# The gate's two experts by two maxima instead of by ranks from all pairs

## The chip, the core and the metric

The kernel runs on one core of one Trainium2 chip. The metric is the device time of one execution in microseconds, as the median of the runs shown. Engines are named as the profile names them: PE is TensorE, DVE is VectorE, ACT is ScalarE, POOL is GpSimd, SP is SyncE, whose queue carries nearly all DMAs.

## The reference

Two layers act on an input of 8 x 256 x 32 x 32 (8 images of 1,024 tokens with 256 channels). Layer 0 is a selective state-space scan over 512 channels with 16 states, and then a mixture of experts: for each token a gate gives probabilities over 8 experts, and the two largest choose the experts and weight their outputs. Layer 1 has three small convolutions and a second, smaller scan, and then a feed-forward network on the half of the tokens that a router ranks highest. The part that the change concerns:

```python
logits = xf @ gate_w + gate_b
probs = jax.nn.softmax(logits, axis=-1)
top2_vals, top2_idx = jax.lax.top_k(probs, 2)
cw = jnp.zeros((N, Ee), dtype=xf.dtype).at[jnp.arange(N)[:, None], top2_idx].add(top2_vals)
```

`top_k` takes the expert with the lower index where two probabilities are equal.

## The kernel before

Layer 0's scan is cut into 16 units, each one image half (512 tokens); four units are a group of 2,048 tokens. A unit is normalized, projected and convolved (`norm`, `project`, `rows_of`, `dt_of`), and then scanned (`scan_unit`, which calls `scan_pair` for every pair of states and each block of 128 channels). One `scan_pair` is, for two states: one POOL multiplication of 128x1024 (L821), two exponentials on ACT into PSUM (L826), two scans along the tokens on DVE (L829), two copies of the last column on ACT (L833, where a half follows), two DVE multiplications (L834), in some pairs a POOL addition (L838), and the sums on PE (L845). The rows `bc` that it multiplies by come by DMA from DRAM, spread over all partitions; there are four buffers for them.

After a unit's scan, `tokens` projects back, takes statistics and writes the gate's logits for its 512 tokens (with small POOL operations, L955 to L964). After each fourth unit, `route` works on the 2,048 tokens of the group. They lie as 128 partitions x 16 blocks, with 8 expert columns each: a tile of 128x128, `[P, NB, E]`. `route` makes a softmax (L983 to L992), finds the two experts of each token (`better` and `masks`, L997 to L1016), counts tokens by expert on PE (`counts`, L1021), gives each token a slot for each of its experts (`sums`, `ends`, `ends2`, `pick`), and turns the gate weights for the bias sum (`chosen`, L1081). All of its tiles lie in one buffer of 1,024 columns, `r`, through the helper `small`. Columns 384 to 767 hold three masks of 128 columns: `sel` (either of the two), `sel1` (the first) and `sel2` (the second).

`better` compares, for two blocks at a time (hence 8 parts), each of the 8 probabilities of a token with each of the other 8: greater than, equal, equal and of lower index (by the constant `first`), the sum of both, and the sum over the others, which is the rank. `masks` makes rank below 1.5, rank below 0.5, and their difference. All of it is on DVE.

Behind a routing come, for its group, `scatter` (token rows to their slots by indirect DMA from POOL, L1113), `experts` (23 blocks of 256 slots, with two DMAs of weights for each block, L1172, and matmuls L1202 and L1224), `combine` (gathers by POOL's indirect DMA, L1300, and the weighted sum), and then layer 1: `taps_of`, `mamba_in`, `mamba_scan` (`scan_pair` again), `mamba_out`, `assemble`, `ranks`, `feed_forward` and `finish`. The work of one group overlaps the scans of later units. For the last group nothing is left to overlap with but the group before it.

The order on every engine is made by a planner when the kernel is built (`Flow`). Each step is declared with `step(engine, us, prio, run, reads, writes, ...)`: an estimated cost, a priority, and the buffers that it reads and writes. The planner picks step after step by priority among those that are ready by its own clock, and hands out buffers from pools; the priorities of later stages come from a table, `PLAN`. Where PE would stand idle for over 0.7 us by this clock, `warm` puts up to eight multiplications by a tile of zeros there (L560 and L564), about one for each 0.3 us. The engines then run their instructions in that order.

Of the kernel before, what the change touches and what calls it, by code (L numbers as in the profile page):

```python
# [31 lines left out]
ALU = mybir.AluOpType  # L32
AX = mybir.AxisListType
# [3 lines left out]
P = 128  # L37
# [5 lines left out]
E, HE = 8, 512  # L43
# [4 lines left out]
NB = 16  # L48
# [46 lines left out]
PE, ACT, DVE, POOL, SP = "PE", "ACT", "DVE", "POOL", "SP"  # L95
# [100 lines left out]
class Flow:  # L196
# [6 lines left out]
    def step(self, engine, us, prio, run, reads=(), writes=(), fills=(), claims=(), table=None, lat=0.0, scan=False):  # L203


        bufs = list(dict.fromkeys([*reads, *writes, *fills, *claims]))
        fresh = list(dict.fromkeys([*writes, *fills, *claims]))
        s = Step(engine, us * (PACE if engine == PE else 1.0), prio, run, table, lat, bufs, fresh)
        for b in fresh:
            b.first = min(b.first, (prio, len(self.steps)))  # L210
        s.scan = scan
        for b in reads:
            assert b.writers or b.slot is not None, "read before it is written"
            s.needs.update(b.writers)
        for b in writes:
            s.needs.update(b.writers, b.readers)
        for b in reads:
            b.readers.append(s)
        for b in (*writes, *fills):
            b.writers.append(s)  # L220
        for b in bufs:
            b.left += 1
        self.steps.append(s)
        return s
# [96 lines left out]
def layers(g, ctx, x, a, out):  # L321
    tc, nc = g.tc, g.nc
    w = ctx.enter_context(tc.tile_pool(name="w0", bufs=1))
# [66 lines left out]
    gsum = g.t(w, [P, 1, E], "gsum")  # L390


    first = g.t(w, [P, E, E], "first")
    nc.gpsimd.memset(first, 0.0)
    for e in range(1, E):
        nc.gpsimd.memset(first[:, e, :e], 1.0)

    earlier = g.t(w, [P, P], "earlier")
    nc.gpsimd.memset(earlier, 1.0)
    nc.gpsimd.affine_select(  # L400
# [9 lines left out]

    count = g.t(w, [P, NX], "count")
    nc.vector.tensor_tensor_scan(count, ones[:, :NX], ones[:, :NX], -1.0, ALU.mult, ALU.add)

    carry = g.t(w, [P, E, NB], "carry")
    nc.gpsimd.memset(carry, 1.0)
# [49 lines left out]
    step, dma = flow.step, flow.dma  # L465
# [67 lines left out]
    def buf(name, line=None):  # L533
        b = Buf(pool[name], line)
        if line is not None:
            line.bufs.append(b)
        return b
# [16 lines left out]
    wide = still.unsqueeze(1).to_broadcast([P, N // P, P])  # L554
# [413 lines left out]
    def route(n, prio):  # L968

        grp = groups[n]  # L970
        wide = [P, NB, E]
        r, lg = buf("sq"), grp["logits"]

        def small(shape, at):

            dims = " ".join("abc"[: len(shape) - 1])
            size = dict(zip("abc", shape[1:]))
            n = 1
            for m in shape[1:]:
                n *= m  # L980
            return r.v[:, at : at + n].rearrange(f"p ({dims}) -> p {dims}", **size)
# [9 lines left out]
            nc.vector.reciprocal(tot, tot)  # L991
            nc.vector.tensor_tensor(lg.v, lg.v, tot.to_broadcast(wide), ALU.mult)  # L992


        part_of = [P, NB // 8, E, E]

        def better(part):  # L997
            blks = slice(part * NB // 8, (part + 1) * NB // 8)
            gt, eq = small(part_of, 128), small(part_of, 256)
            mine = lg.v[:, blks].unsqueeze(3).to_broadcast(part_of)  # L1000
            other = lg.v[:, blks].unsqueeze(2).to_broadcast(part_of)
            nc.vector.tensor_tensor(gt, other, mine, ALU.is_gt)
            nc.vector.tensor_tensor(eq, other, mine, ALU.is_equal)
            nc.vector.tensor_tensor(eq, eq, first.unsqueeze(1).to_broadcast(part_of), ALU.mult)
            nc.vector.tensor_tensor(gt, gt, eq, ALU.add)
            nc.vector.tensor_reduce(small(wide, 0)[:, blks], gt, AX.X, ALU.add)

        def sels():
            return [small(wide, 384 + 128 * i) for i in range(3)]

        def masks():
            rank = small(wide, 0)
            sel, sel1, sel2 = sels()
            nc.vector.tensor_scalar(sel, rank, 1.5, None, ALU.is_lt)
            nc.vector.tensor_scalar(sel1, rank, 0.5, None, ALU.is_lt)
            nc.vector.tensor_tensor(sel2, sel, sel1, ALU.subtract)  # L1016


        pt, pw = banks(2)
# [66 lines left out]
        step(DVE, 0.4, prio, softmax, [], [r, lg])  # L1086
        step(ACT, 0.25, prio, lambda: nc.scalar.activation(lg.v, lg.v, AF.Exp), [], [lg], table="exp")
        step(DVE, 0.6, prio + 0.5, softmax2, [], [r, lg])
        for part in range(8):
            step(DVE, 1.9, prio + 1 + 0.25 * part, lambda part=part: better(part), [lg], [r])  # L1090
        step(DVE, 0.6, prio + 3, masks, [], [r])
        step(PE, 0.5, prio + 3, counts, [r], [pt])
        step(DVE, 1.7, prio + 3.5, sums, [pt], [r])
        step(DVE, 0.8, prio + 4, ends, [], [r])
# [637 lines left out]
    for i, s in enumerate(UNIT_AT):  # L1732
        if i == 0:
            unit_prep(0)
        dt_of(i, 1, s + 4)
        if i + 1 < len(units):
            fetch_x(i + 1, s)
        scan_unit(i, s)
        if i + 1 < len(units):
            unit_prep(i + 1)  # L1740
        end = s + 2 * DS
        tokens(i, end + 1)
        if i % 4 == 3:
            n = i // 4
            at = PLAN[n]
            route(n, end + 12)
            scatter(n, end + 16, at["put"])
            experts(n, *at["experts"])
            combine(n, *at["combine"])
            taps_of(n, *at["taps"])  # L1750
            m = at["mamba"]
            mamba_in(n, m - 26, m + 5)
            mamba_scan(n, m)
            mamba_out(n, m + DS + 2)
            assemble(n, *at["assemble"])
            ranks(n, at["ranks"])
            feed_forward(n, *at["ffn"])
            finish(n, *at["finish"])
# [4 lines left out]
@with_exitstack  # L1763
def kernel(ctx: ExitStack, tc: tile.TileContext, a: dict, out: bass.AP):
    nc = tc.nc
    g = Ctx(tc)
    const = ctx.enter_context(tc.tile_pool(name="const", bufs=1))
    g.dram = ctx.enter_context(tc.tile_pool(name="dram", bufs=1, space=DRAM))
    g.psum = ctx.enter_context(tc.tile_pool(name="ps0", bufs=1, space=PSUM))
    g.ident = g.t(const, [P, P], "ident")  # L1770
    make_identity(nc, g.ident)
    g.mean256 = g.t(const, [P, P], "mean256")
    nc.gpsimd.memset(g.mean256, 1.0 / C)

    def column(value, tag):
        t = g.t(const, [P, 1], tag)
        nc.gpsimd.memset(t, value)
        return t

    g.one = column(1.0, "one")  # L1780
    g.eps5 = column(1e-5, "eps5")
    g.eps6 = column(1e-6, "eps6")
    g.eps_vim = column(1e-5 * 1e-6, "eps_vim")
    layers(g, ctx, a["x"], a, out)
# [122 lines left out]
```

## Time and profile before

| | us |
|---|---|
| median of 3 runs (lowest to highest) | 3680.02 (3673.19 to 3691.26) |
| the profiled execution | 3683.03 |
| its span | 3681.0 |
| DVE busy | 2918.0 |
| the scans' two DVE lines, L829 and L834, mean of one | 1.22 to 1.28, and 0.69 |
| ACT table loads | 166 of 1.283 |
| granted PE clock, mean | 0.946 |

The four routings begin (first instruction of `softmax`, L985) at 666.7, 1279.8, 1932.2 and 2825.9 us from the start of the span. The last instruction of the fourth (L1083) starts at 2899.2; from 2902 to the end of the span are 779 us. A profile line names the kernel's line, the engine, the operation, what it writes and reads, its shape and its count; then its busy time and mean, and after the bar the time that the engine stood idle just before it.

### The profile page before, as it was taken

The numbers are of one execution on the slowest core, as the hardware profiler recorded it, in microseconds if no ns is written. First come the engines' busy times: TensorE is split into PE (matmuls) and PEld (weight loads), VectorE is DVE, ScalarE is ACT, GpSimd is POOL, SyncE is SP. The second block draws the span as 40 slices with busy tenths as digits, with TensorE's granted clock in tenths as the row PEclk, the third lists the DMA queues.
The fourth block names the chain that finished last, engine by engine and source line by source line (L and its number), as shares of the span: only waits on it lengthen the run. The fifth ranks groups of instructions, "written<-read, shape, count | busy, mean of one in ns | idle before, by whom it ended". The sixth has DMA issues, their size and how long they took to land. (4 is left out here: it accounts for less than half of the span.)

```text
span 3681.0 us, 37497 instructions
## 1 busy us (share of the span) xinstructions
PE 3211.1 (87%) x10567; PEld 1807.2 (49%) x10567; DVE 2918.0 (79%) x4181; ACT 2188.2 (59%) x3985; POOL 2407.4 (65%) x1751
## 2 busy tenths in 40 slices
PE   8889888889889988978998898988888888899858
PEld 3334333334445444444554445555546565685536
DVE  4889889989778987986988789768698938965951
ACT  4555455467567656755875675655675546747533
POOL 3767567487867758986986887654786743716522
PEclk9999999999999999999999999999999988999989
DMA  6334333346445445644654557565657786877756
GB/s 231 132 132 138 110 125 129 107 161 209 159 133 172 167 134 174 203 155 147 211 178 164 179 178 240 190 197 161 195 180 261 234 258 206 307 230 244 265 168 190
DMA packets 276301, 676.61 MB, mean 184 GB/s; under 512 B 31015, under 2 KB 114861, under 8 KB 276094
## 3 DMA queue, kind: packets, MB, share of 16 engines
q1 hardware_dynamic: 257662, 623.87, 51.6%
q0 software_dynamic: 18432, 50.36, 4.2%
q8 instruction: 84, 1.38, 0.2%
q14 instruction: 123, 1.01, 0.1%
HBM read 572.92 MB, written 101.19 MB: 183 GB/s over the span
## 5 line engine op out<-in xcount | busy, mean ns | idle before, releaser
L821 POOL TENSOR_TENSOR dbu<-dtx,bc 128x1024 f32<-128x1024 f32 x551 | 1300.8, 2374 | 239.7 <-PE y L845 119.6
L845 PE MATMUL y<-dbu,ident 128*128 128x512 f32 x1616 | 837.4, 630 | 174.9 <-POOL dbu L838 129.5
L826 ACT ACTIVATE mm<-dt,neg_a 128x512 f32<-128x512 f32 x1152 | 767.7, 688 | 172.9 <-DVE dbu L834 150.6
L829 DVE TENSOR_TENSOR_SCAN mm<-mm,dbu 128x512 f32<-128x512 f32 x566 | 691.9, 1222 | 211.3 <-ACT mm L826 176.7
L834 DVE TENSOR_TENSOR dbu<-mm,bc 128x512 f32<-128x512 f32 x1104 | 763.3, 691 | 53.1 <-PE mm L1202 0.5
L829 DVE TENSOR_TENSOR_SCAN mm<-mm,state,dbu 128x512 f32<-128x512 f32 x560 | 717.6, 1281 | 40.0 <-ACT mm L826 25.4
L838 POOL TENSOR_TENSOR dbu<-dbu 128x512 f32<-128x512 f32 x318 | 412.0, 1296 | 294.6 <-DVE dbu L834 277.6
L845 PEld LDWEIGHTS y<-dbu,ident 128*128 128x128 f32 x1616 | 291.5, 195 | 537.8 <-issue 211.9
L833 ACT COPY state<-mm 128x1 f32<-128x1 f32 x576 | 91.8, 160 | 701.3 <-DVE dbu L834 660.6
L1224 PE MATMUL mm<-we,hid 128*128 128x256 f32 x1536 | 370.6, 394 | 34.3 <-ACT hid L1208 23.2
L1202 PE MATMUL mm<-xbt,we 128*128 128x256 f32 x1632 | 384.1, 386 | 17.9 <-ACT xbt L1190 10.3
L1202 PEld LDWEIGHTS mm<-xbt,we 128*128 128x128 f32 x1632 | 312.0, 193 | 106.1 <-issue 30.9
L1224 PEld LDWEIGHTS mm<-we,hid 128*128 128x128 f32 x1536 | 296.6, 197 | 116.0 <-ACT hid L1208 35.5
L756 PE MATMUL mm<-pre,w_tap 128*128 128x512 f32 (+3 forms) x512 | 245.2, 622 | 28.8 <-ACT pre L743 27.7
L1300 POOL DMA_INDIRECT ys<-slots_y,slot x128 | 126.9, 992 | 184.8 <-DMA xb<-slots_t 71.3
L560 PE MATMUL y<-still 128*128 128x512 bf16 x924 | 237.5, 392 | 0.0
L462 ACT ACT_TABLE_LOAD x166 | 213.0, 1283 | 3.0
L1208 ACT ACTIVATE hid<-mm,we 128x256 f32<-128x256 f32 x408 | 161.5, 475 | 33.9 <-PE mm L1202 25.1
L756 PEld LDWEIGHTS mm<-pre,w_tap 128*128 128x128 f32 x512 | 97.3, 197 | 167.2 <-issue 106.1
L1688 POOL DMA_INDIRECT ys<-y,slot_t x64 | 64.2, 1003 | 172.8 <-DVE xc L1698 81.0
L560 PEld LDWEIGHTS <-still 128*128 128x128 bf16 x924 | 92.6, 101 | 159.5 <-issue 93.0
L1113 POOL DMA_INDIRECT slots_x<-xg,slot x120 | 122.4, 1020 | 30.8 <-issue 19.7
(279 smaller groups left out, 4476.7 us busy)
## 6 DMA issues: line engine op xcount, KB each, us to landing
bc<-rows SPq DMA_DIRECT2D x610, 512.0 KB
we<-in_W SPq DMA_DIRECT2D x82, 514.0 KB
we<-in_W SPq DMA_DIRECT2D x77, 512.0 KB
xb<-slots_x SPq DMA_DIRECT2D x92, 256.0 KB
slots_y<-xo SPq DMA_DIRECT2D x92, 256.0 KB
xc<-x SPq DMA_DIRECT2D x64, 256.0 KB
we<-in_W12f SPq DMA_DIRECT2D x20, 514.0 KB
slots_x<-xg SPq DMA_DIRECT2D x10, 1024.0 KB
```

The costliest lines, as they stand in the source:

```text
L462: nc.scalar.preload_act_table_set(tables[name])
L560: nc.tensor.matmul(live[0].v[:, 0], still, wide, start=False, stop=False)
L756: nc.tensor.matmul(tc_.v[:, cut:], w_tap[:, c, j], pre.v[:, cut + j : j + N], start=j == 3, stop=j == 0)
L821: gpsimd(2.45, prio, lambda: nc.gpsimd.tensor_tensor(dbu.v, dtxs.v[:, n : n + 1].to_broadcast(wide2), bt.v, ALU.mult), [dtxs, bt], [dbu], ...
L826: step(ACT, 0.69, prio, lambda j=j, h=h: nc.scalar.activation(h.v, dts.v[:, n], AF.Exp, scale=scales(j)), [dts], [h], table="exp", scan=True)
L829: step(DVE, 1.25, prio, lambda j=j, h=h: nc.vector.tensor_tensor_scan(h.v, h.v, dbu.v[:, j], 0.0 if initial is None else initial[1](j), AL ...
L834: step(DVE, 0.68, prio, lambda j=j, h=h: nc.vector.tensor_tensor(dbu.v[:, j], h.v, ct.v[:, j], ALU.mult), [h, ct], [dbu], scan=True)
L838: gpsimd(1.3, prio + 2.3, lambda: nc.gpsimd.tensor_tensor(dbu.v[:, 0], dbu.v[:, 0], dbu.v[:, 1], ALU.add), [], [dbu])
L845: nc.tensor.matmul(y.v[:, n], g.ident, dbu.v[:, j], start=False, stop=stop and (paired or j == 1))
L1202: nc.tensor.matmul(tv[:, f], we[0].v[:, at : at + P], xbt.v[:, k], start=k == 0, stop=k == KC - 1)
L1208: nc.scalar.activation(hid.v[:, f], tv[:, f % 2], func, bias=we[0].v[:, at : at + 1])
L1224: nc.tensor.matmul(to, hid.v[:, f, h * P : (h + 1) * P], we[1].v[:, f * C : (f + 1) * C], start=extra is None and f == 0, stop=f == FC - 1,)
```

## The change

`better`, `masks` and `first` go. In their place `choose(i)` runs twice in a routing, once for each expert: the maximum over the 8 columns, equality with it, multiplication by `turn_of` (8 for expert 0 down to 1 for expert 7), the maximum of that, and equality with it, which is one column of ones in each token, at the first of equals. The second time it works on a copy in which 2 is subtracted at the expert already chosen, and it ends by adding both masks into `sel`. `turn_of` is made once, at the start, from `count`. In the planner, eight steps of 1.9 and one of 0.6 become one of 1.4 and one of 1.9.

```diff
-    first = g.t(w, [P, E, E], "first")
-    nc.gpsimd.memset(first, 0.0)
-    for e in range(1, E):
-        nc.gpsimd.memset(first[:, e, :e], 1.0)
-
@@
+    turn_of = g.t(w, [P, 1, E], "turn_of")
+    nc.vector.tensor_scalar(turn_of[:, 0], count[:, :E], -1.0, float(E), ALU.mult, ALU.add)
@@
-        part_of = [P, NB // 8, E, E]
-
-        def better(part):
-            blks = slice(part * NB // 8, (part + 1) * NB // 8)
-            gt, eq = small(part_of, 128), small(part_of, 256)
-            mine = lg.v[:, blks].unsqueeze(3).to_broadcast(part_of)
-            other = lg.v[:, blks].unsqueeze(2).to_broadcast(part_of)
-            nc.vector.tensor_tensor(gt, other, mine, ALU.is_gt)
-            nc.vector.tensor_tensor(eq, other, mine, ALU.is_equal)
-            nc.vector.tensor_tensor(eq, eq, first.unsqueeze(1).to_broadcast(part_of), ALU.mult)
-            nc.vector.tensor_tensor(gt, gt, eq, ALU.add)
-            nc.vector.tensor_reduce(small(wide, 0)[:, blks], gt, AX.X, ALU.add)
@@
-        def masks():
-            rank = small(wide, 0)
+        def choose(i):
+
+            left, one, same = small(wide, 128), small([P, NB, 1], 0), small(wide, 256)
             sel, sel1, sel2 = sels()
-            nc.vector.tensor_scalar(sel, rank, 1.5, None, ALU.is_lt)
-            nc.vector.tensor_scalar(sel1, rank, 0.5, None, ALU.is_lt)
-            nc.vector.tensor_tensor(sel2, sel, sel1, ALU.subtract)
+            if i:
+                nc.vector.scalar_tensor_tensor(left, sel1, -2.0, lg.v, ALU.mult, ALU.add)
+            val, to = (left, sel2) if i else (lg.v, sel1)
+            nc.vector.tensor_reduce(one, val, AX.X, ALU.max)
+            nc.vector.tensor_tensor(same, val, one.to_broadcast(wide), ALU.is_equal)
+            nc.vector.tensor_tensor(same, same, turn_of.to_broadcast(wide), ALU.mult)
+            nc.vector.tensor_reduce(one, same, AX.X, ALU.max)
+            nc.vector.tensor_tensor(to, same, one.to_broadcast(wide), ALU.is_equal)
+            if i:
+                nc.vector.tensor_tensor(sel, sel1, sel2, ALU.add)
@@
-        for part in range(8):
-            step(DVE, 1.9, prio + 1 + 0.25 * part, lambda part=part: better(part), [lg], [r])
-        step(DVE, 0.6, prio + 3, masks, [], [r])
+        for i in range(2):
+            step(DVE, 1.4 + 0.5 * i, prio + 1 + i, lambda i=i: choose(i), [lg], [r])
```

## The prediction

> **What bounds the kernel now.** I read the page's totals and slices first, then the busy time of each engine in the stretches around the four routings, then the groups of the lines that go, then the timeline of one of them.
>
> ```profile
> span 3681.0 us, 37497 instructions
> PE 3211.1 (87%) x10567; PEld 1807.2 (49%) x10567; DVE 2918.0 (79%) x4181; ACT 2188.2 (59%) x3985; POOL 2407.4 (65%) x1751
> DVE  4889889989778987986988789768698938965951
> ```
>
> PE looks busiest, but 237.5 us of it is L560, the idle-filling multiplies by zero of `warm`, so its real load is near that of VectorE (DVE), 79%. No one engine bounds the whole. The question is what bounds the stretches where the routing stands: core time, then busy time of PE, PEld, DVE, ACT and POOL, granted clock, DMA share and GB/s.
>
> ```profile
> 660.00:745.00 85.00, 67.97 (x167) 27.18 (x166) 79.15 (x131) 36.93 (x76) 34.64 (x22) 0.94 0.29 95
> 1285.00:1375.00 90.00, 74.46 (x217) 37.13 (x217) 80.39 (x130) 48.51 (x94) 49.18 (x31) 0.92 0.39 126
> 1970.00:2050.00 80.00, 68.75 (x222) 38.50 (x221) 67.48 (x123) 47.71 (x105) 49.18 (x47) 0.98 0.49 162
> 2815.00:2915.00 100.00, 80.61 (x322) 57.66 (x320) 91.87 (x130) 54.31 (x98) 56.13 (x47) 0.95 0.73 243
> 2902.00:3036.00 134.00, 110.85 (x489) 84.15 (x489) 72.94 (x145) 70.19 (x141) 79.67 (x105) 0.92 0.76 245
> ```
>
> In the first two DVE works 93% and 89% of the time while ACT and POOL are at 41% to 55%: DVE sets the pace. In the third it is at 84%. In the fourth it is at 92%, but PE (81%, hardly any of it filler) and DMA (0.73) are near their limits too. The last row is what follows the fourth routing: DVE at 54%, PE 83%.
>
> Now the lines that go (busy us, mean ns, idle before):
>
> ```profile
> L1002 DVE TENSOR_TENSOR sq<-logits 128x128 f32<-128x128 f32 x32 | 21.9, 683 | 0.7
> L1004 DVE TENSOR_TENSOR sq<-sq,first 128x128 f32<-128x128 f32 x32 | 19.5, 610 | 1.1
> L1003 DVE TENSOR_TENSOR sq<-logits 128x128 f32<-128x128 f32 x32 | 18.8, 587 | 0.0
> L1005 DVE TENSOR_TENSOR sq<-sq 128x128 f32<-128x128 f32 x32 | 12.5, 389 | 1.1
> L1006 DVE TENSOR_REDUCE sq<-sq 128x16 f32<-128x128 f32 x32 | 9.2, 286 | 1.1
> L1016 DVE TENSOR_TENSOR sq<-sq 128x128 f32<-128x128 f32 x4 | 2.1, 531 | 0.1
> ```
>
> The means of the first four are up to twice their medians (284 to 292 ns), the reduce's is not (285 to 289 ns in all 32). The timeline of the first routing says why:
>
> ```profile
> 683.57 1.80 DVE L1002 TENSOR_TENSOR sq<-logits 128x128 f32<-128x128 f32 x1
> 685.29 2.43 DVE L1003 TENSOR_TENSOR sq<-logits 128x128 f32<-128x128 f32 x1
> 687.76 0.29 DVE L1004 TENSOR_TENSOR sq<-sq,first 128x128 f32<-128x128 f32 x1
> ...
> 682.88 4.71 POOL L821 TENSOR_TENSOR dbu<-dtx,bc 128x1024 f32<-128x1024 f32 x2 [4.83 <-DMA bc<-rows]
> 698.38 4.66 POOL L821 TENSOR_TENSOR dbu<-dtx,bc 128x1024 f32<-128x1024 f32 x2 [10.79 <-DMA bc<-rows]
> ```
>
> While POOL multiplies (682.88 to 687.59), a DVE instruction with two SBUF operands ends only with POOL's; after that it takes 0.29. The scan's own L829 and L834, which have one operand in PSUM, keep 1.22 and 0.69 us throughout.
>
> **What is removed.** 4 routings x 8 parts x 5 instructions, and three mask instructions per routing: 21.9 + 19.5 + 18.8 + 12.5 + 9.2 + 2.1 and 0.9 + 0.9 for L1014 and L1015 = 85.8 us of DVE. By line and stretch it is 18.1, 19.7, 22.7 and 25.3 us for the four. At bare durations it would be 32 x 1.47 (four parts in a row from 692.41 to 698.28) + 4 x 0.6 = 49.4; the other 36 us are waits for POOL.
>
> **What is added.** Per routing 12 instructions of 128x128: four reduces, seven TENSOR_TENSOR and one SCALAR_TENSOR_TENSOR, all but the reduces with two SBUF operands. No row has that last form; L1612 (128x128, 348 ns) and L1698 (128x256, 516 ns) bound it, and it goes with the others. Bare: 4 x 0.286 + 8 x 0.291 = 3.5 us. With POOL in the way, the mean over the 132 removed two-operand instructions is (72.7 + 2.1) / 132 = 0.567: 1.1 + 8 x 0.567 = 5.7. Such instructions that stand alone between scan steps, as L1083 (826 ns) and L986 (899 ns), suffer most: 1.1 + 8 x 0.9 = 8.3. I take 5.7, because the new ones come in runs of five and seven as the old came in runs of five. Four routings: 22.8, bounds 14 and 33. Net on DVE: 85.8 - 22.8 = 63.0 us less, bounds 53 and 72; by routing 12.4, 14.0, 17.0, 19.6.
>
> The Trainium skill speaks against the trade in one place: "VectorE: DVE Perf Modes", section "Rules for kernel authors", calls the reduce along the free axis the slowest DVE operation and advises restructuring it away; the trace has it at 0.286 us beside 0.284 to 0.292 for the TENSOR_TENSOR, and unstretched. The page gives no factor; if a reduce cost twice its row, the 16 new ones would add 4.6 us.
>
> At the start, eight POOL memsets of `first` go (0.14 + 7 x 0.09 us) and one DVE instruction on 8 elements comes (0.17, as L1065). DVE idles 5.06 us before 15.98 us anyway, and POOL's fills have no reader waiting: nothing; without that cover, 0.2 us more at most, or 0.8 less.
>
> **What lies on the path.** No wait is added: `choose` follows on DVE what `better` followed. Behind it stand the count matmuls (L1023), the slots, the scatter and the experts, and between them the scan steps, which is why the end moves at all: DVE comes back to L829 sooner. But the kernel's planner orders everything from declared costs, and these fall from 8 x 1.9 + 0.6 to 1.4 + 1.9 per routing, so it deals all queues anew. I compared the order of the instructions. Until the first routing PE is the same, and after it the interleaving stays close: the fourth routing ends after 1,080 scans in both programs, with 121 fewer DVE instructions before it and 842 against 844 behind. Expert matmuls against scan steps stand alike. So the old schedule with shorter routings is a fair model. Two differences cost: three more table loads on ACT (3 x 1.283 = 3.8 us, which I price at nothing since ACT is 41% idle; 3.8 if that cover is gone), and behind the fourth routing 16 more expert matmuls (16 x 0.39 = 6.3 us) and 26 more filler multiplies, each of which stands for 0.3 us of idle PE in the plan (7.8).
>
> What share becomes time is my choice, by stretch. Routings one and two: 0.85, a little under DVE's share, giving 10.5 and 11.9. Routing three, where DVE already waits: 0.6, giving 10.2. Routing four: PE and DMA have their own work to finish, and 19.6 - 6.3 - 7.8 leaves 5.5; I take 0.4, 7.8. Sum: 40.4 us. The profiled execution took 3683.0 (span 3681.0 and 2 us around it), 3 us above the median of the runs; 3683.0 - 40.4 = 3642.6, and against the median 3680.0 it is 3640.
>
> **Rivals.**
> - *All of it passes.* DVE is the pace everywhere, and the new instructions meet POOL rarely: 72 us, 3608. For it: the first two stretches. Against: the fourth, and DVE at 54% after it.
> - *Absorbed.* The scan loop is held by its row loads: in the first stretch POOL's L821 waits 10.79 us at 698.38 for `bc`, which L834 must first have freed. If that wait or PE takes over each time, a fifth passes: 63 x 0.2 = 13, 3667. Against: the load itself is released by DVE.
> - *Slower: a gather blocks POOL in the tail.* The combine gathers (L1300) stand in POOL's one queue behind expert outputs, and once that queue sat 71.3 us:
>
> ```profile
> L1300 POOL DMA_INDIRECT ys<-slots_y,slot x128 | 126.9, 992 | 184.8 <-DMA xb<-slots_t 71.3
> ```
>
>  In the newly dealt tail a second such wait, with the last group's scan multiplies behind it, would give 3640 + 71 = 3711. It makes the kernel slower by over 0.5% from 40 + 18 = 58 us on. Against: POOL's scatters and gathers stand after nearly the same numbers of scan multiplies as before.
> - That the change doesn't do what it says is excluded: the built program has 123 fewer DVE instructions, 172 out and 49 in.
>
> **How the numbers follow.** Forecast 0.50, all of it 0.20, absorbed 0.16, slower 0.14. A measurement of this kernel can tell about 0.5% (18 us) from no change: below 3662 is faster, above 3698 slower. So faster 0.70, same 0.16, slower 0.14. The range runs from just under the rival with all of it, 3604, to 3694, which takes in the absorbed case and a small loss, and leaves out the blocked queue; on its own the forecast would be 3620 to 3660.
>
> **What would show it.** DVE busy near 2918 - 63 = 2855, in 4058 instructions; the routing's new lines at 5.7 us each time, with stretched TENSOR_TENSORs and unstretched reduces. The second routing's first reduce (L985) some 10 us sooner, the third's some 22, the fourth's (2825.9) some 33, and the end some 40. I am wrong if the fourth comes as predicted and the tail, 779 us from 2902 to the end, has grown by more than 20; or if the routings shrink and the next ones don't come sooner; or if the new instructions take over 33 us.

## Result and the profile after

The changed kernel takes 3679.33 us (median of 12 runs, 3670.7 to 3689.88) beside 3678.7 us (12 runs, 3670.96 to 3691.26) for the kernel before on the same chip: a ratio of 1.0003, 95% interval 0.9992 to 1.0014. None of the 40 us that were forecast came. The profiled execution took 3687.6, span 3685.5, at a mean granted PE clock of 0.944.

The page's totals of the changed kernel:

```profile
span 3685.5 us, 37366 instructions
PE 3218.3 (87%) x10568; PEld 1812.4 (49%) x10568; DVE 2868.3 (78%) x4058; ACT 2191.3 (59%) x3988; POOL 2391.3 (65%) x1746
```

DVE has 49.7 us less to do (2918.0 to 2868.3), in the 4,058 instructions expected, and the span is none the shorter: DVE's idle time rose from 763 to 817 us. Line numbers ahead of `choose` are 2 lower in the changed kernel and in those made from it: the scan L829 is L827, its multiplication L834 is L832, the exponential L826 is L824, and POOL's L821 is L819. The instructions of `choose`, from the same trace's groups (busy us and mean ns after the bar, then the idle time before them):

```profile
L1004 DVE TENSOR_TENSOR sq<-sq,turn_of 128x128 f32<-128x128 f32 x8 | 9.4, 1173 | 0.3
L1003 DVE TENSOR_TENSOR sq<-logits,sq 128x128 f32<-128x128 f32 x4 | 7.4, 1848 | 0.1
L1006 DVE TENSOR_TENSOR sq<-sq 128x128 f32<-128x128 f32 x8 | 5.7, 718 | 0.3
L1003 DVE TENSOR_TENSOR sq<-sq 128x128 f32<-128x128 f32 x4 | 3.6, 889 | 0.1
L1005 DVE TENSOR_REDUCE sq<-sq 128x16 f32<-128x128 f32 x8 | 2.3, 286 | 0.3
L1000 DVE SCALAR_TENSOR_TENSOR sq<-sq,logits 128x128 f32<-128x128 f32 x4 | 1.1, 286 | 0.1
```

With the first reduce (L1002, 2.2 us) and the sum of both masks (L1008, 1.2), the new lines take 32.9 us, 8.2 per routing. All of the TENSOR_TENSORs but L1008 have means of 718 to 1,848 ns, while the reduces keep 280 to 286, and so does the operation that the trace before did not have (L1000): 286, under the 348 ns that the prediction took as its lower bound, though none of the four stood beside a multiplication of POOL here (one did in e13, and took 0.71 us). So the work was taken away: 85.8 - 32.9 is 53 us net, of which 2 went to the softmax's L984 (5.6 us; as L986 it took 3.6) and the rest is DVE's shrinkage within 1.2 us.

To see where it stopped being worth anything, the two traces are divided at the same scan instructions, by their count, so that each row spans the same share of the scans: the four routings, and the stretch behind the fourth. The columns are start and end, core time, then busy time and instructions of PE, PEld, DVE, ACT and POOL, granted clock, DMA share and GB/s. First the kernel before:

```profile
645.49:726.63 81.14, 66.49 (x167) 27.09 (x166) 76.18 (x128) 34.55 (x74) 35.58 (x23) 0.94 0.32 107
...
1271.75:1353.66 81.91, 68.68 (x205) 34.84 (x204) 76.00 (x116) 41.48 (x85) 47.71 (x31) 0.92 0.44 145
...
1898.77:2024.58 125.81, 110.17 (x381) 66.30 (x381) 107.89 (x187) 72.94 (x173) 89.62 (x73) 0.97 0.50 161
...
2798.58:2909.05 110.47, 92.55 (x374) 68.06 (x373) 97.24 (x142) 62.97 (x111) 59.18 (x43) 0.95 0.75 250
2909.05:3124.13 215.08, 181.05 (x752) 128.61 (x750) 136.32 (x343) 120.05 (x228) 104.68 (x124) 0.90 0.72 228
```

The changed kernel:

```profile
643.00:720.90 77.90, 63.45 (x163) 26.01 (x161) 72.37 (x103) 32.27 (x72) 35.72 (x23) 0.96 0.35 118
...
1266.30:1336.39 70.09, 56.15 (x168) 27.47 (x167) 64.12 (x93) 35.38 (x77) 43.94 (x29) 0.89 0.42 139
...
1893.73:2022.73 129.00, 110.73 (x376) 65.50 (x376) 96.76 (x157) 73.60 (x175) 89.56 (x75) 0.96 0.48 156
...
2792.12:2885.97 93.85, 76.92 (x302) 55.27 (x300) 77.10 (x108) 51.90 (x90) 48.05 (x34) 0.91 0.73 252
2885.97:3114.83 228.86, 199.82 (x825) 138.53 (x826) 154.56 (x358) 132.99 (x249) 111.43 (x135) 0.93 0.73 234
```

The first, second and fourth rows are shorter by 3.2, 11.8 and 16.6 us, the third is longer by 3.2, and the row behind the fourth is longer by 13.8. PE's counts tell why the second and the fourth are no plain gains: the fourth has 374 matmuls before and 302 after, and the row behind it 752 and 825, so 72 matmuls have only moved to the other side of the line. The stretch behind the second routing, up to scan 610, likewise went from 163.6 us with 449 matmuls to 169.6 with 472. So the routings begin (L985, now L983) at 664.2, 1274, 1927 and 2819 us, only 2.5, 5.5, 5.4 and 6.5 sooner, and the 2.5 stand ahead of the first routing, where the change has hardly anything. From the end of the fourth row to the end of the span it is 799.5 us instead of 772.

What DVE's scans wait for over the whole run of the kernel before (us, times, longest):

```profile
DVE mm L829 <- ACT mm L826: 203.2, 120, 7.4
DVE mm L829 <- POOL dbu L821: 23.8, 17, 4.5
```

The same waits in the changed kernel:

```profile
DVE mm L827 <- ACT mm L824: 221.9, 124, 11.6
DVE mm L827 <- POOL dbu L819: 38.2, 18, 8.6
```

The scans wait 18.7 us longer for the exponentials, and 14.4 longer for POOL's multiplication. That is a first sign of where the gain went: DVE comes back sooner to a scan whose input is not there yet. It is no more than a sign, since two executions of one program, e1 and e16 below, differ by 14 us in the first of these sums (227.5 and 213.5).

### The profile page after: what moved, and what is told of

Same layout as the page of the kernel before. It is cut to its first block, busy times and chain, and to the rows that moved or that the text cites. A ratio compares the mean times of both kernels' runs of the same rounds, so it can differ in the third digit from the quotient of the medians.

```text
span 3685.5 us, 37366 instructions
## 1 busy us (share of the span) xinstructions
PE 3218.3 (87%) x10568; PEld 1812.4 (49%) x10568; DVE 2868.3 (78%) x4058; ACT 2191.3 (59%) x3988; POOL 2391.3 (65%) x1746
## 5 line engine op out<-in xcount | busy, mean ns | idle before, releaser
L819 POOL TENSOR_TENSOR dbu<-dtx,bc 128x1024 f32<-128x1024 f32 x547 | 1288.0, 2367 | 242.2 <-PE y L843 115.1
L827 DVE TENSOR_TENSOR_SCAN mm<-mm,dbu 128x512 f32<-128x512 f32 x566 | 691.9, 1222 | 237.8 <-ACT mm L824 186.4
L824 ACT ACTIVATE mm<-dt,neg_a 128x512 f32<-128x512 f32 x1152 | 766.9, 688 | 171.3 <-DVE dbu L832 149.5
L832 DVE TENSOR_TENSOR dbu<-mm,bc 128x512 f32<-128x512 f32 x1108 | 765.7, 691 | 54.0 <-DVE mm L827 0.5
L827 DVE TENSOR_TENSOR_SCAN mm<-mm,state,dbu 128x512 f32<-128x512 f32 x560 | 717.6, 1281 | 45.6 <-ACT mm L824 31.7
L1193 PE MATMUL mm<-xbt,we 128*128 128x256 f32 x1616 | 385.8, 390 | 15.3 <-DVE dbu L832 6.8
L1291 POOL DMA_INDIRECT ys<-slots_y,slot x128 | 126.9, 992 | 178.7 <-DMA slots_y<-xo 68.5
L558 PE MATMUL y<-still 128*128 128x512 bf16 x878 | 226.9, 393 | 0.0
```

Of the source, the lines that this page charges most:

```text
L558: nc.tensor.matmul(live[0].v[:, 0], still, wide, start=False, stop=False)
L819: gpsimd(2.45, prio, lambda: nc.gpsimd.tensor_tensor(dbu.v, dtxs.v[:, n : n + 1].to_broadcast(wide2), bt.v, ALU.mult), [dtxs, bt], [dbu], ...
L824: step(ACT, 0.69, prio, lambda j=j, h=h: nc.scalar.activation(h.v, dts.v[:, n], AF.Exp, scale=scales(j)), [dts], [h], table="exp", scan=True)
L827: step(DVE, 1.25, prio, lambda j=j, h=h: nc.vector.tensor_tensor_scan(h.v, h.v, dbu.v[:, j], 0.0 if initial is None else initial[1](j), AL ...
L832: step(DVE, 0.68, prio, lambda j=j, h=h: nc.vector.tensor_tensor(dbu.v[:, j], h.v, ct.v[:, j], ALU.mult), [h, ct], [dbu], scan=True)
L1193: nc.tensor.matmul(tv[:, f], we[0].v[:, at : at + P], xbt.v[:, k], start=k == 0, stop=k == KC - 1)
```

## The experiments

Two things changed at once, the instructions and, through their declared costs, the order on all engines. The first four kernels take these apart. All ratios are against the kernel before on the same chip, with 95% intervals; each expectation says what its theories are.

**e1: the new instructions in the old order.** The planner is told the old costs, so that it deals as before; `choose` runs in the first and the last of the eight steps, and the others are empty.

```diff
-        for i in range(2):
-            step(DVE, 1.4 + 0.5 * i, prio + 1 + i, lambda i=i: choose(i), [lg], [r])
+        for part in range(8):
+            step(DVE, 1.9, prio + 1 + 0.25 * part, lambda part=part: choose(part // 7) if part in (0, 7) else None, [lg], [r])
+        step(DVE, 0.6, prio + 3, lambda: None, [], [r])
```

> The changed decision (two maxima) in the order of the kernel before: the planner is told eight steps of 1.9 and one of 0.6 as before, the first and the last of the eight run the two maxima and the others nothing. All other instructions stand in the order of before on every engine. Theory A (the newly dealt order ate the gain): about 40 us faster than before, 3640. Theory B (the time saved on DVE is not on the path, whatever the order): within 15 us of before, DVE idle up by about what its busy time falls.

Measured: 3654.77, ratio 0.9973 (0.9961 to 0.9984), which is 10 us. The same work in the new order gave nothing, so the order matters; but even in the old order, which the prediction took as its model, a quarter of the forecast arrives. Theory A's 40 us are out, and the time lies within theory B's 15 us. Its rows, divided as above:

```profile
642.81:717.80 74.99, 63.69 (x170) 26.07 (x169) 67.65 (x98) 34.47 (x74) 35.67 (x23) 1.00 0.35 116
...
1259.09:1336.02 76.93, 67.33 (x207) 34.25 (x206) 66.44 (x85) 41.36 (x85) 47.77 (x31) 0.96 0.45 154
...
1880.11:2008.56 128.45, 111.25 (x381) 66.86 (x381) 97.00 (x157) 73.82 (x175) 89.49 (x75) 0.96 0.48 158
...
2778.93:2883.02 104.09, 91.25 (x374) 67.47 (x373) 80.23 (x111) 62.76 (x111) 58.84 (x43) 0.97 0.81 270
2883.02:3092.00 208.98, 179.58 (x752) 127.49 (x750) 136.46 (x343) 120.27 (x228) 105.24 (x124) 0.92 0.73 235
```

The counts on PE stay as before (374 and 752), so here a row's length can be read. The four routings have 8.5, 9.6, 10.9 and 17.0 us less DVE work, 46 us, and are 6.2, 5.0, -2.6 and 6.4 us shorter, 15 us: a third. The third routing gives back nothing at all. (The rows are those of one execution each; e16, the same program on another chip, repeats these four as 74.7, 77.0, 128.6 and 105.5.)

**e2: the old instructions in the new order.** The kernel before, with its comparisons in two steps of four parts each, declared at 1.4 and 1.9.

```diff
-        for part in range(8):
-            step(DVE, 1.9, prio + 1 + 0.25 * part, lambda part=part: better(part), [lg], [r])
-        step(DVE, 0.6, prio + 3, masks, [], [r])
+        def half(i):
+            for part in range(4 * i, 4 * i + 4):
+                better(part)
+            if i:
+                masks()
+
+        for i in range(2):
+            step(DVE, 1.4 + 0.5 * i, prio + 1 + i, lambda i=i: half(i), [lg], [r])
```

> The comparisons of all pairs in the order of the changed kernel: two steps declared at 1.4 and 1.9, which run four parts each, the second the masks too. All other instructions stand in the order of after. Theory A: 35 to 50 us slower than after, 3715 to 3730, since the order costs 40 and nothing is saved. Theory B: within 15 us of after.

Measured: 3703.15, 1.0104 (1.0088 to 1.0119), 38 us slower. That is theory A's distance to the changed kernel, but not its reason: A has the order cost 40 us whatever the work. With e1 and the changed kernel this makes a square: the new order costs 1.04% with the old work and 0.3% with the new, and the new work is worth 1.0% in the new order and 0.27% in the old. The two do not add up, so "what the instructions save" has no value of its own apart from where they stand.

**e3: each comparison twice, in the old order.**

```diff
-            step(DVE, 1.9, prio + 1 + 0.25 * part, lambda part=part: better(part), [lg], [r])
+            step(DVE, 1.9, prio + 1 + 0.25 * part, lambda part=part: (better(part), better(part)), [lg], [r])
```

> The kernel before with every comparison made twice (the same values written again), in the order of before: 160 more DVE instructions, 82 us at the rows of before, 49 bare. Theory A (DVE sets the pace at the routings): 45 to 80 us slower, 3725 to 3760. Theory B in its simple form (slack on DVE): under 20 us slower.

Measured: 3722.84, 1.0166 (1.0147 to 1.0185), 61 us slower, inside theory A's 45 to 80. By the rows, 14.3, 14.3, 12.2 and 9.5 us more DVE work made the routings 15.2, 15.5, 16.2 and 13.0 us longer. More work costs at least its full length, and less work (e1) brings a third of it. Such a kink suggests that part of the work before stood in gaps that it just about filled.

One gap can be seen in the trace. Around the third routing of the kernel before, this is ACT (start, duration, line; waits in brackets):

```profile
1962.28 0.70 ACT L826 ACTIVATE mm<-dt,neg_a 128x512 f32<-128x512 f32 x1
1962.99 1.28 ACT L1208 ACT_TABLE_LOAD   x1
...
1966.41 1.28 ACT L737 ACT_TABLE_LOAD   x1
...
1981.38 1.28 ACT L462 ACT_TABLE_LOAD   x1
...
1983.12 0.67 ACT L826 ACTIVATE mm<-dt,neg_a 128x512 f32<-128x512 f32 x1
```

Between two exponentials of the scan (L826) lie 20.1 us, in which ACT loads another table for the experts' activation, another for L737, and returns to the first; its other instructions here belong to the experts, the combine, the next unit and layer 1. The three loads are 3.8 us of the hole, and for some 7 us ACT waits in it for PE. DVE's scans have no input for that time. What DVE does in it:

```profile
1964.27 0.69 DVE L834 TENSOR_TENSOR dbu<-mm,bc 128x512 f32<-128x512 f32 x1
1964.88 0.59 DVE L1002 TENSOR_TENSOR sq<-logits 128x128 f32<-128x128 f32 x1
1965.40 2.43 DVE L1003 TENSOR_TENSOR sq<-logits 128x128 f32<-128x128 f32 x1
...
1983.91 0.29 DVE L1016 TENSOR_TENSOR sq<-sq 128x128 f32<-128x128 f32 x1
1984.12 1.22 DVE L829 TENSOR_TENSOR_SCAN mm<-mm,dbu 128x512 f32<-128x512 f32 x1
```

It has the comparisons to do: 17.2 of this routing's 22.7 us stand in that hole, DVE is busy for 19.2 of its 20.1 us, and the next scan (1984.12) follows right behind the last mask, 0.3 us after the exponential that it needs has ended (1983.12 + 0.67). The same hole in e1:

```profile
1948.39 0.69 DVE L832 TENSOR_TENSOR dbu<-mm,bc 128x512 f32<-128x512 f32 x1
1958.44 0.75 DVE L1333 BATCH_NORM_STATS2 bn<-xo 128x6 f32<-128x256 f32 x2 [9.36 <-ACT xo L1327]
...
1963.65 0.29 DVE L1008 TENSOR_TENSOR sq<-sq 128x128 f32<-128x128 f32 x1
1968.02 1.23 DVE L827 TENSOR_TENSOR_SCAN mm<-mm,dbu 128x512 f32<-128x512 f32 x1 [4.08 <-POOL rs L901]
```

ACT's hole is 20.1 us again, and DVE is busy for 7.2 of them: it waits 9.36 us for the expert output of which it takes statistics, and 4.08 us before the next scan (the trace names a POOL event as its releaser, but the exponential that the scan reads ran from 1967.24 to 1967.91). What was removed had been standing where DVE had nothing else to do. Outside the hole this routing's choice of experts took 5.5 us before and takes 6.3 in e1 (4.4 of its 10.7 us lie in the hole), so nothing of the 12 us saved could show.

**e4, e10, e11: the changed kernel with other declared costs.**

```diff
-            step(DVE, 1.4 + 0.5 * i, prio + 1 + i, lambda i=i: choose(i), [lg], [r])
+            step(DVE, 3.4 + 1.4 * i, prio + 1 + i, lambda i=i: choose(i), [lg], [r])
```

and 2.4 + 1.0 * i in e10, 5.0 + 2.0 * i in e11.

> The changed kernel with the two steps declared at 3.4 and 4.8, which is what they measured (8.2 us for a routing), instead of 1.4 and 1.9: the same instructions, one more deal of the order. Theory A: deals differ by some 10 to 30 us, so this one lands between 3640 and 3700, and not on 3680 but by chance. Theory B: within 10 us of after.

> The changed kernel with the two steps declared at 2.4 and 3.4: the same instructions, another deal. If deals scatter without regard to how true the declared costs are, it lies anywhere from 0.4% under before to 0.2% over; if truer costs make better deals, between the change (1.4 and 1.9: +0.03%) and the deal at 3.4 and 4.8 (-0.33%).

> The changed kernel with the two steps declared at 5.0 and 7.0, more than they take: a third deal. Scatter: anywhere from -0.4% to +0.2%. Truer costs make better deals: worse than the deal at 3.4 and 4.8.

Measured: e10 (2.4 and 3.4) 3653.51, 0.9958 (0.9942 to 0.9973); e4 (3.4 and 4.8) 3655.32, 0.9967 (0.9955 to 0.9979); e11 (5.0 and 7.0) 3652.86, 0.9968 (0.9956 to 0.9979). All three beat both kernels by 0.3 to 0.4%, with the same instructions as the changed kernel. The two steps together measured 8.2 us per routing, of which the change declared 3.3; the three declare 5.8, 8.2 and 12.0. There is no trend among them, so truer declarations did not make better orders here. Whether 3.3 gives a poor order because it is too low, or by chance, one point cannot tell.

**e12: the changed kernel again**, on the chip of e9 to e11.

> The changed kernel itself, beside the other deals on one chip: within 0.15% of before, as it was.

Measured: 3667.45, 1.0000 (0.9987 to 1.0013). So the difference to e10 and e11 is not one between chips. Its fourth routing and the stretch behind it:

```profile
2789.95:2885.54 95.59, 80.03 (x302) 57.47 (x300) 77.20 (x108) 51.86 (x90) 47.53 (x34) 0.88 0.72 243
2885.54:3102.56 217.02, 197.88 (x823) 138.51 (x824) 152.69 (x358) 131.15 (x248) 109.91 (x134) 0.94 0.76 243
```

Beside e1 the fourth is 8.5 us shorter and the next row 8.0 longer: as in the first trace of this kernel, PE's matmuls moved across the line (302 and 823). Its span is 15.3 us above e1's (on two chips whose kernels before both took 3667.0), and these lie in no one place. Divided at the same scans, the differences are +8.1 up to the second routing, -6.8 and +5.6 in it and behind it, +3.8 from there to the third, -0.3 from the third to scan 1120 with all that moved across the fourth, and +5.0 behind that. From the fourth's end to the end of the span it has 778.5 us; the 799.5 of the other trace of this same program was partly that execution's own.

**e5, e6: the new deal in the fourth routing alone, and in the first three alone.** The other routings are declared as in e1.

```diff
+        if n == 3:
             for i in range(2):
                 step(DVE, 1.4 + 0.5 * i, prio + 1 + i, lambda i=i: choose(i), [lg], [r])
+        else:
+            for part in range(8):
+                step(DVE, 1.9, prio + 1 + 0.25 * part, lambda part=part: choose(part // 7) if part in (0, 7) else None, [lg], [r])
+            step(DVE, 0.6, prio + 3, lambda: None, [], [r])
```

(`n < 3` in e6.)

> The two maxima in all four routings; the first three are declared to the planner as before (eight steps of 1.9, one of 0.6), the fourth as in the change (1.4 and 1.9), so the order is the old one up to the fourth routing and newly dealt behind it. Theory C (what ate the gain is the new deal of the stretch behind the fourth routing, where after took 799 us from that routing's end against 772 before): 0 to 0.3% slower than before. Theory D (the deals of the first three routings did it): faster by 0.3% or more, as the run in the old order.

> The opposite: the first three routings declared as in the change, the fourth as before. Theory C: faster than before by 0.3% or more. Theory D: no faster than after, 0 to 0.3% slower than before. If both this and its counterpart are faster, or both slower, the deal is a lottery and neither place is to blame.

Measured: e5 3675.49, 0.9992 (0.9979 to 1.0005); e6 3669.94, 0.9979 (0.9966 to 0.9991). Beside e1's 0.9973 the fourth's new deal costs 0.19% and the other three's 0.06%, which together are about the 0.3% that the new deal costs in the changed kernel. Theory D's values lie outside both intervals, and theory C's reach into both. That points at the fourth, but the intervals of e5 and e6 overlap, so it is not settled.

**e7, e8: the changed kernel and the kernel before without the fillers of `warm`**, since the changed one has 26 more behind the fourth routing.

```diff
-WARM = True
+WARM = False
```

> The changed kernel with the planner's filler multiplies (L560, L564) left out; the rest of the order is that of after. Theory F (the 26 more fillers behind the fourth routing, and fillers planned for gaps that the chip doesn't have, cost PE time where PE is near its limit): 15 to 35 us faster than after. Theory G (the fillers do what they are for, and PE's granted clock falls without them): 1% or more slower, with a lower granted clock.

> The kernel before with the filler multiplies left out. Theory F: 5 to 20 us faster than before, less than the changed kernel gains, since it has fewer behind the fourth routing. Theory G: 1% or more slower, as with the changed kernel.

Measured: e7 3690.48, 1.0042 (1.0025 to 1.0058), and e8 3688.93, 1.0020 (1.0005 to 1.0036). The fillers do not cost the changed kernel its gain: both kernels are slower without them, by 0.2 to 0.4%, while the mean granted PE clock falls from 0.946 to 0.899 in the kernel before and from 0.944 to 0.900 in the changed one. They are worth something, less than the expectation that had put them at a per cent.

**e9: no decision at all, in the old order.** Three mask instructions on a constant, in the last step.

```diff
+        def fixed():
+            sel, sel1, sel2 = sels()
+            turns = turn_of.to_broadcast(wide)
+            nc.vector.tensor_scalar(sel, turns, E - 1.5, None, ALU.is_gt)
+            nc.vector.tensor_scalar(sel1, turns, E - 0.5, None, ALU.is_gt)
+            nc.vector.tensor_tensor(sel2, sel, sel1, ALU.subtract)
...
+            step(DVE, 1.9, prio + 1 + 0.25 * part, lambda part=part: fixed() if part == 7 else None, [lg], [r])
```

> The order of before, and no decision at all: the masks are made by three instructions that send every token to experts 0 and 1 (the comparisons and maxima are left out, all else runs). It takes a further 33 us of DVE from the run in the old order with two maxima (36.6 us of decision there, 3 here). Theory H (what went lay in holes of the exponential stream, while ACT loads other tables and works on other functions, and those holes keep their length): the third routing's hole of 20.1 us and its stretch of 126 to 128 us stay, the others shrink by under 4 us each, in all 0 to 10 us less than with the two maxima, 0.2 to 0.5% under before. Theory L (DVE's time passes in part everywhere): 0.32 x 33 = 11 us to 25 us less, evenly over the four, 0.6 to 1% under before.

Measured: 3638.57, 0.9921 (0.9901 to 0.994), 29 us faster than before and 0.52% (19 us) faster than e1 by the ratios, for 25.0 us less of DVE. At 0.79% below the kernel before it is past the 0.2 to 0.5% of the expectation's theory H, which as put there is not upheld, and inside the 0.6 to 1% of theory L: the last 25 us pay better than the 50 before them did. By the rows, though, the four routings shrink by 3.8, 2.4, 4.7 and 0.4 us beside e1, 11 us of it, for 26.8 us of DVE less in them; the rest came in other stretches. The third's hole is 20.1 us in this trace too, as theory H had it; what H overlooked is that 6.3 of e1's 10.7 us stood outside it, and the row is 4.7 shorter. All tokens now go to the same two experts, so later stages do not see the same data, and how much of the rest is due to that was not tried.

That left it open whether place is what makes the work cheap, or only a general share of any DVE work passes. The last four runs put the same work at two places of one routing, on one chip.

**e13 to e16: idle work in and behind the third routing's hole.** To e1 are added reduces of the logits into a scratch column: 38 in the third step of the third routing, ahead of the wait of 9.36 us shown above (e13); 76 there (e14); 38 ahead of `sums`, some 20 DVE instructions later, where the scans run again (e15). e16 is e1 again. The rest of the order is the same in all four.

```diff
+        def extra(times):
+            for _ in range(times):
+                nc.vector.tensor_reduce(small([P, NB, 1], 0), lg.v, AX.X, ALU.max)
...
-            step(DVE, 1.9, prio + 1 + 0.25 * part, lambda part=part: choose(part // 7) if part in (0, 7) else None, [lg], [r])
+            step(DVE, 1.9, prio + 1 + 0.25 * part, lambda part=part: choose(part // 7) if part in (0, 7)
+                 else extra(38) if n == 2 and part == 2 else None, [lg], [r])
```

> The kernel of e1 (two maxima in the old order) with 38 extra reduces of 128x128 (38 x 0.325 = 12.4 us of VectorE) in the third routing's empty third step, ahead of the batch norm L1333 at which VectorE idled 9.36 us in the hole of the exponentials, and 4.08 us after it. Theory H (work in a hole of the exponentials is free up to the idle time in it, 13.4 us here): +0 to +2 us beside e1, ratio to the kernel before as e1's, about 0.997. Theory P (some third of any VectorE work passes, wherever it stands): +4 us, 0.998. Theory D (all of it passes, as in e3): +12 us, 1.000.

> As e13 with 76 reduces (24.7 us) at the same place. Theory H: the first 13.4 us are free and the rest passes in full, +11 us beside e1, 1.000. Theory P: +8 us, 0.9995. Theory D: +25 us, 1.004. Beside e13, H expects a kink: nothing for the first 12 us and 9 to 11 us for the next 12.

> The kernel of e1 with the same 38 reduces 20 instructions later on VectorE, ahead of the third routing's L1020, where the exponentials run again and VectorE had no idle time for some 15 us. Theory H: +12 us beside e1, 1.000, 10 to 12 us above e13 though the work is the same. Theory P: +4 us, as e13. Theory D: +12 us, as e13.

> The kernel of e1 again, on the chip of e13 to e15, as the base they are set against: 0.996 to 0.998 by every theory.

Measured:

| | extra DVE work | median, us | ratio (95%) |
|---|---|---|---|
| e16 | none | 3666.68 | 0.9966 (0.9953 to 0.9979) |
| e13 | 12.1 us in the hole | 3664.73 | 0.9958 (0.9942 to 0.9975) |
| e14 | twice that in the hole | 3672.1 | 0.9981 (0.9968 to 0.9994) |
| e15 | 12.1 us behind the hole | 3678.15 | 1.0002 (0.9991 to 1.0014) |

The third routing's row (scans 770 to 805) of each, first e16:

```profile
1886.67:2015.28 128.61, 111.49 (x380) 67.06 (x381) 97.02 (x156) 73.03 (x173) 89.14 (x73) 0.95 0.48 157
```

e13, with the work in the hole:

```profile
1878.37:2007.12 128.75, 111.39 (x381) 66.80 (x381) 105.87 (x195) 73.90 (x175) 89.60 (x75) 0.96 0.48 157
```

e14, with twice the work there:

```profile
1878.46:2015.21 136.75, 113.44 (x379) 68.30 (x380) 116.08 (x233) 73.86 (x175) 89.55 (x75) 0.91 0.45 148
```

e15, with e13's work behind the hole:

```profile
1884.94:2025.98 141.04, 112.57 (x381) 67.97 (x381) 107.70 (x194) 73.75 (x175) 89.90 (x75) 0.92 0.44 143
```

128.6, 128.8, 136.8 and 141.0 us. The same 12.1 us cost 0.1 us in the hole and 12.4 just behind it. (DVE's busy time in the row grows by 8.9 and 10.7 us, since some instructions no longer stand beside a multiplication of POOL.) PE's granted clock is lower in the two long rows, but PE is busy for only 1 to 2 us more in them, so that is not what made them longer. What e13's DVE does in the hole, and then e15's reduces, behind it:

```profile
1946.69 0.69 DVE L832 TENSOR_TENSOR dbu<-mm,bc 128x512 f32<-128x512 f32 x1
1947.30 12.14 DVE L1013 TENSOR_REDUCE sq<-logits 128x16 f32<-128x128 f32 x38
1959.36 0.74 DVE L1338 BATCH_NORM_STATS2 bn<-xo 128x6 f32<-128x256 f32 x2
...
1966.31 1.23 DVE L827 TENSOR_TENSOR_SCAN mm<-mm,dbu 128x512 f32<-128x512 f32 x1 [3.42 <-POOL rs L901]
```

```profile
1982.32 12.14 DVE L1013 TENSOR_REDUCE sq<-logits 128x16 f32<-128x128 f32 x38
```

In e13 the reduces run from 1947.30 to 1959.44, the statistics find their input ready, and the next scan comes 19.62 us after the last multiplication ahead of the hole (1946.69 to 1966.31), as in e1, where it was 19.63 (1948.39 to 1968.02). In e14 the hole's idle time is used up, and of the second 12.1 us 8.0 come through. Some 11 were expected; the hole held more room than the two waits' 13.4 us, since L1003, which took 2.70 us in e1 beside POOL's multiplication, comes after it in e13 and takes 0.29. In e14 DVE works without a break from the first reduce to the next scan, and ACT's hole grows with it from 20.1 to 27.6 us, because the next exponential stands behind L896, which waits 7.47 us for the statistics that DVE makes behind the reduces. By the medians e15 is 13.4 us slower than e13. For this hole the theory of the holes stands. A general share falls, since it asks the same of e13 and e15, and so does the theory that all DVE work costs its length.

## Why the prediction was wrong

- **What is removed, and the counts: right.** The lines went, 4,058 instructions are left, the three added table loads are there (358 on all lines against 355; the 166 of the table above are one line's, L462, and are now 169), and the reduces are unstretched at 0.28 to 0.29 us, no more than a bare TENSOR_TENSOR. The Trainium skill's page "VectorE: DVE Perf Modes", section "Rules for kernel authors", calls them the slowest DVE operation; for these f32 tiles the trace does not agree.
- **What is added: at its upper bound.** 8.2 us per routing instead of 5.7. The step took the mean over all removed instructions, 0.567, because the new ones "come in runs of five and seven"; but the removed ones stood up to six parts in a row, of which most were bare, and the new runs fall into POOL's multiplications with a greater share: 22 of the 132 removed two-operand instructions took over 0.35 us, and 11 of the 32 new ones. The net was 53 us by line instead of 63.
- **"What share becomes time": the step that failed.** 0.85, 0.85, 0.6 and 0.4 were read from DVE's busy share. In the old order the rows showed 0.72, 0.52, nothing and 0.38, and the clock showed 10 us of 40. In the third, DVE was busy because the planner had laid 17.2 of the 22.7 us of this very work into a hole of ACT's exponentials of 20.1 us. A busy share with the work in it does not say what the stretch takes without it. That is shown for the third alone; why the other three passed on 0.38 to 0.72 was not traced. The prediction saw that DVE waits there, and lowered the share to 0.6; the right value was none. Of the forecast 40.4 us, by one execution of each kernel, 11.7 went with the costlier new lines (the prediction's shares of e1's 46.0 us would be 28.7) and 13.8 with the shares (the rows gave 14.9); between these 14.9 and the 10 by the ratio lie 5 that no row explains.
- **"The old schedule with shorter routings is a fair model": failed too.** With the old schedule the kernel is 10 us faster (e1). The new deal took that back, about 0.3% between e1 and the changed kernel, and as much shows against e4, e10 and e11. The comparison of orders counted scans and matmuls on each side of the fourth routing, and the two differences it priced, 6.3 and 7.8 us, were only moved across the line. In all, PE has 1,128 fillers instead of 1,127. Where the 11 us lie was not found; e5 and e6 point at the fourth routing and the traces at several places. A single trace can hardly show it: from the fourth routing's end on, seven executions that all have the old order there (before, e1, e3, e13 to e16) take 758 to 783 us.
- **The rivals.** "Absorbed" had the right size in the old order (13 us, and 10 were measured), but its reason is not shown: it named row loads or PE, and in the third routing it was ACT. POOL's multiplication waited 101.7 us for the row loads before, 98.4 in the changed kernel, and 111.0 and 95.9 in the two executions of e1's program, which shows no growth beyond their spread. A second long wait of the gathers did come, but not one of 71 us. L1300 had waits of 71.3 and 25.2 us before; as L1291 in the changed kernel it has

```profile
POOL ys L1291 <- DMA slots_y<-xo: 68.5, 1, 68.5
POOL ys L1291 <- DMA xc<-x: 35.1, 1, 35.1
```

  In the four traces with the change's deal of the fourth routing (the changed kernel, e2, e5, e12) the shorter wait is 30.5 to 35.1 us, in four with the old one (before, e1, e6, e16) 18.2 to 25.2. That would be about the size of what the new deal cost, but e11 has 29.4 and is fast, so it is not shown.
- **The signs named beforehand.** "The routings shrink and the next ones don't come sooner" is what happened: the fourth came 6.5 us sooner instead of 33. The new lines' 32.9 us stay just under the 33 named.

## What to carry to other kernels

Before pricing work that is taken off a busy engine, look at what the engine would do in that moment instead: if its next instruction waits for another engine that is itself switched to something else, the work can be free up to the length of that wait, as 12.1 us were here, and taking it away brings nothing. Look at the stream that feeds the loop (here the exponentials) for its gaps, and split the work by whether it lies in one. And where an order is dealt from declared costs, time a change of instructions in the old order and the new one apart: a change of a declared number is a change of its own, and a few values of it are worth trying.

## What was not expected of the hardware

Of the changed kernel's TENSOR_TENSORs of 128x128 in SBUF, the eleven of L1003, L1004 and L1006 that ran beside a multiplication of POOL took 1.2 to 2.7 us, four to nine times the 0.29 of the others, and reduces of the same tile, beside it, kept 0.27 to 0.29. Thirty-eight reduces in a row took 12.14 us, 0.32 each. And without the 1,127 fillers the mean granted PE clock is lower by 5% (0.946 to 0.899, e8), but the kernel only 0.2% slower; since PE also had less to do (3070 us instead of 3211), this is not the price of the clock alone.
